# Attention weighting by seven half-wide products in place of eight, with x reread at the end of attention: one change to a fused attention and cluster-MLP kernel

## The chip, the cores and the metric

The kernel runs on one core of one Trainium2 chip. The metric is the device time of one execution in microseconds (us), as a median of several executions. The profile is that of one execution, taken by the hardware profiler. The engines are called by their short names: PE is TensorE's matmul (PEld is the load of its weights), DVE is VectorE, ACT is ScalarE, POOL is GpSimd, SP is SyncE, which here only issues DMAs. L513 is line 513 of the kernel before.

## The reference

Four images of 256 channels and 64 x 64 = 4096 positions go through two layers. The first is self-attention:

```python
q = jnp.einsum('oc,bcn->bno', wq, xf) + bq                  # 32 channels
k = jnp.einsum('oc,bcn->bon', wk, xf) + bk[None, :, None]   # 32 channels
attn = jax.nn.softmax(jnp.einsum('bnd,bdm->bnm', q, k), axis=-1)
v = jnp.einsum('oc,bcn->bon', wv, xf) + bv[None, :, None]   # 256 channels
out = jnp.einsum('bcn,bmn->bcm', v, attn).reshape(B, Cc, H, W)
return gamma[0] * out + x
```

The second layer normalises its input over the whole image (group norm with one group), adds a context-cluster block to it, normalises again, adds an MLP (256 to 1024, gelu, back to 256), and ends with two batch norms with relu and a 256 x 256 pointwise convolution between them. All is in float32.

The change is in the first layer: in the products of v with the softmax weights, in the addition of x, and in the statistics of the sum that the second layer needs.

## The kernel before, in words

**Stages.** Images are worked one after the other, each in three stages: attention (`weighting`, L619), the cluster block (`cluster`, L732) and the MLP (`mlp`, L1199). The order of instructions on every engine is the order in which the program writes them (`manual_schedule`); nothing reorders them. The projections of the next image (q, k and v from its x) are a list of small steps, which a "filler" hands out within the cluster block and the MLP of the image before. The next image's first eight units of scores are also made inside the MLP before it.

**Units.** Attention is divided into 8 blocks of 512 queries (`nb`) and 8 groups of 512 keys (`g`), so into 64 units `u = 8 nb + g`. A key group is four key tiles of 128. For each unit:

- `score` (L383): four matmuls, one for each key tile (L395), give scores of 128 keys x 512 queries. They lie in two PSUM buffers of two key tiles each (pool `ps_s`, L76). ACT copies both to an SBUF tile of the pool `spool` (L417, L422), and DVE takes a running maximum over the keys straight from PSUM (L421, L424; in group 0 one operation, L419).
- `exps` (L492): DVE subtracts the maximum (L500), ACT takes the exponential (L503), both in place, in two halves of two key tiles, and POOL adds the weights up in `acc` (L505, L508).
- `weigh` (L510): 16 recorded PE instructions of 512 columns (L513). A float32 matmul is recorded as two instructions; there are four key tiles and two halves of the channels (`KC`), so eight products. The sums stay in two PSUM banks `av` (pool `ps_a`, L77) over all eight groups of a block.

Scores are made ten units ahead (`LEAD`); ten slots of `spool` and one other tile hold them. What happens in which unit is written out by hand in `weighting`: each unit has four "quarters", one key tile each, and the table `at` (L606, L610) with `due` (L612) says in which unit and quarter the scores of a later unit are made. That is one unit's scores for one unit of weighting, except in an image's first six units, where the lead is caught up: there eight units' scores (seven in image 0) are due, one every 2.8 quarters (3 in image 0).

**Maximum and sum of a block.** The maximum of the next block is folded (`fold`, L429) and reduced across the partitions on DVE (`highest`, L473, called at the end of group 5), goes to DRAM and comes back as a row on all partitions (`everywhere`, L82), and is copied to a PSUM tile (`known`, L482, at the end of group 6), from which the subtractions read it. The sum of the weights of a finished block is taken in the same way in the next block (`gather`, L525; `total`, L532).

**Output of a block.** `clear` (L527) copies the two `av` banks to SBUF with the factor gamma. In the next block `add` (L541) multiplies by the reciprocal of the sum and adds x in place, both on POOL. x of the image lies in four tiles of `spool` throughout attention; ACT adds the bias gamma*bv to it once (`biased`, L622, L671). `seen` (L552) and `pooled` (L557) then take the statistics and the pooled cells that the cluster block needs, one block in each block of time. The tiles of the next image's x are loaded (`load_x`, L88) as slots come free, in the last units. For the last block the sum goes over PE (`den`, `inv`, from L686 on) with some filler steps between.

**PSUM.** There are eight banks: four in `ps_s` (two buffers of two banks), two in `ps_a`, two in `ps_m` (L78; maximum, projections and others).

Of the kernel before, what the change touches and what calls it, by code (L numbers as in the profile page):

```python
# [14 lines left out]
P = 128  # L15
B, C, H, W = 4, 256, 64, 64
N = H * W
# [13 lines left out]
LEAD, SLOTS = 10, 10  # L31

# [14 lines left out]
def attention_then_cluster_block(  # L47
# [23 lines left out]
    spool = ctx.enter_context(tc.tile_pool(name="spool", bufs=N // XT + SLOTS))  # L71
# [144 lines left out]
    def derived():  # L216
# [18 lines left out]
        tps = ps_m.tile([P, NB], F32, tag="m", name="wf_p")  # L235
# [50 lines left out]
    def attention(b, xs):  # L286
# [53 lines left out]
        def keys(i):  # L340

            ps = ps_m.tile([P, NB], F32, tag="m", name=f"kp_{b}_{i}")
            parts = [
                big.tile([P, NB], F32R, tag="k", bufs=2, name=f"hl{j}_{b}_{i}") for j in range(2)
            ]
            projected("k", i, ps)
            halves_of("k", i, *parts, ps)
# [35 lines left out]
        def score(u, hooks=None, later=None):  # L383

            nb, g = divmod(u, GRP)
            if u + 1 < units:
                k_unit(u + 1)
            q_s, k_s = qs[nb], ks.pop(u)
            pool, tag = (swap, "w1") if u % (SLOTS + 1) == SLOTS else (spool, "s")
            s = slots[u] = pool.tile([P, RG, NB], F32, tag=tag, name=f"s_{b}_{u}")  # L390
            halves = [
                ps_s.tile([P, 2, NB], F32, tag="s", name=f"sc_{b}_{u}_{h}") for h in range(2)
            ]
            for r in range(RG):
                nc.tensor.matmul(  # L395
                    halves[r // 2][:, r % 2, :],
                    k_s[:, r * P : (r + 1) * P],
                    q_s,
                    start=True,
                    stop=True,  # L400
                )
            if g == 0:
                tops[nb] = work.tile([P, 2, NB], F32, tag="top", bufs=1, name=f"top_{b}_{nb}")
            top = tops[nb]
            if hooks is not None:

                nc.scalar.copy(s[:, 0:2, :], halves[0])
                hooks.append(lambda: nc.scalar.copy(s[:, 2:4, :], halves[1]))
                for h in range(1 if g == 0 else 0, 2):
                    for i in range(2):  # L410
                        later.append(
                            lambda h=h, i=i: nc.vector.tensor_tensor(
                                top[:, i], s[:, i] if g == 0 else top[:, i], s[:, 2 * h + i], ALU.max
                            )
                        )
                return
            nc.scalar.copy(s[:, 0:2, :], halves[0])  # L417
            if g == 0:
                nc.vector.tensor_tensor(top, halves[1], s[:, 0:2, :], ALU.max)  # L419
            else:  # L420
                nc.vector.tensor_tensor(top, halves[1], top, ALU.max)  # L421
            nc.scalar.copy(s[:, 2:4, :], halves[1])  # L422
            if g:
                nc.vector.tensor_tensor(top, halves[0], top, ALU.max)  # L424
# [28 lines left out]
        def reduced(src, flipped, low, op):  # L453
# [4 lines left out]
            )  # L458
            four = low[:D, D : D + 64].rearrange("p (r c) -> p r c", r=4)
            for r in range(4):  # L460
                nc.vector.tensor_copy(four[:, r], low[r * D : (r + 1) * D, :16])
# [4 lines left out]
            return one  # L466
# [6 lines left out]
        def highest(nb):  # L473
# [3 lines left out]
            one = reduced(top[:, 0], top[:, 1], low, ALU.max)  # L477
# [4 lines left out]
        def known(nb, mb):  # L482
            mxs[nb] = ps_m.tile([P, NB], F32, tag="m", name=f"mb_{b}_{nb}")
            nc.scalar.copy(mxs[nb], mb)  # L484

        def spread(nb, dg):
            mxs[nb] = ps_m.tile([P, NB], F32, tag="m", name=f"mb_{b}_{nb}")
            nc.tensor.matmul(
                mxs[nb], ones, dg.rearrange("p j n -> p (j n)"), start=True, stop=True
            )  # L490

        def exps(u):  # L492
            nb, g = divmod(u, GRP)
            s = slots[u]
            if g == 0:
                accs[nb] = work.tile([P, 2, NB], F32, tag="acc", bufs=1, name=f"acc_{b}_{nb}")
            acc = accs[nb]
            for h in range(2):
                sh = s[:, 2 * h : 2 * h + 2, :]
                nc.vector.tensor_tensor(  # L500
                    sh, sh, mxs[nb].unsqueeze(1).to_broadcast([P, 2, NB]), ALU.subtract
                )
                nc.scalar.activation(sh, sh, AF.Exp)  # L503
            if g == 0:
                nc.gpsimd.tensor_tensor(acc, s[:, 0:2], s[:, 2:4], ALU.add)  # L505
            else:
                for h in range(2):
                    nc.gpsimd.tensor_tensor(acc, acc, s[:, 2 * h : 2 * h + 2], ALU.add)  # L508

        def weigh(u, av, quarter):  # L510
            g = u % GRP
            for c in range(KC):
                nc.tensor.matmul(  # L513
                    av[c],
                    own["v"][:, RG * g + quarter, c * P : (c + 1) * P],
                    slots[u][:, quarter, :],
                    start=(g == 0 and quarter == 0),
                    stop=(g == GRP - 1 and quarter == RG - 1),
                )
# [1183 lines left out]
```

## Time and profile before

| what | us |
|---|---|
| median of three runs | 3288.82 |
| lowest, highest of the three | 3286.51, 3291.25 |
| the profiled execution | 3289.97 |
| its span, from the first to the last instruction | 3287.9 |
| attention of image 0 (76.5 to 574) | 497.5 |
| cluster block of image 0 (574 to 655) | 81.0 |
| MLP of image 0 (655 to 890.5) | 235.5 |

Mean granted clock of PE: 0.994. Attention of images 1 to 3 takes 496.8, 493.5 and 523.0 (in the last a block of the image before is finished).

How to read the page: "busy" is time in which an engine executed; a share is of the span. A group line reads: line, engine, operation, output <- inputs, shape, count | busy us in all, mean ns of one | idle us of the engine just before them, and what ended most of it. The chain that ended last is followed back from the last instruction, at each step to what released it. In a timeline the columns are start, us from the first start to the last end of the instructions taken together, engine, line, and in brackets the idle time before and what ended it. PE's ends are modelled, since matmuls are pipelined: the distance between starts is the rate.

### The profile page before, as it was taken

To read this page: it belongs to the slowest core of one execution; us is meant where nothing else is said; L and a number is where in the kernel's file an instruction comes from. 1 tells how busy PE (TensorE), PEld (TensorE's weight loads), DVE (VectorE), ACT (ScalarE), POOL (GpSimd) and SP (SyncE) were. 2 spreads that over 40 slices of the span, in tenths; PEclk is the share of its full clock that TensorE was granted. 3 is DMA by queue.
4 is the path that set the end of the run, shared out by engine and by line. 5 is a ranking of instruction groups with operands and counts; after the bars stand their busy time and mean duration, and the time that the engine had idled before them with its cause. 6 is when DMAs were issued, how large, how long until landed. Compare 5 with 4: busy or idle time off the path is not lost.

```text
span 3287.9 us, 33084 instructions
## 1 busy us (share of the span) xinstructions
PE 3220.5 (98%) x11114; PEld 1933.6 (59%) x11114; DVE 2232.6 (68%) x3570; ACT 1680.7 (51%) x2254; POOL 1933.1 (59%) x1362
## 2 busy tenths in 40 slices
PE   7999999999999999999999999999999999999999
PEld 4444444788644444478864444457874444446786
DVE  3767774667677777467767776646776777765665
ACT  4655553445565555354556555434556555544444
POOL 0675676366456666636646567654654676673663
PEclk9999999999999999999999999999999999999999
DMA  4111113100111111310011111121011111110000
GB/s 159 52 42 49 49 39 114 36 20 30 42 52 40 47 55 33 114 36 20 30 52 45 48 52 42 45 98 36 30 37 51 51 42 48 45 44 1 14 20 26
DMA packets 87706, 154.78 MB, mean 47 GB/s; under 512 B 13200, under 2 KB 22000, under 8 KB 87536
## 3 DMA queue, kind: packets, MB, share of 16 engines
q1 hardware_dynamic: 86576, 151.55, 14.3%
q8 instruction: 88, 1.44, 0.2%
q10 hardware_dynamic: 832, 1.11, 0.1%
q14 instruction: 82, 0.67, 0.1%
q0 software_dynamic: 128, 0.00, 0.0%
HBM read 118.96 MB, written 33.67 MB: 46 GB/s over the span
## 4 chain that ended last, share of the span: by engine, by line
PE 93%; DVE 4%; ACT 1%; issue 1%; POOL 1%; DMA 0%; SPq 0%; ACTq 0%; DVEq 0%; POOLq 0%
PE av L513 52%; PE mo L1332 10%; PE sc L395 7%; PE hq L1415 5%; PE hp L1415 3%; PE hr L1415 3%; PE fv L911 3%; PE vp L358 3%; PE mo L1316 1%; PE hq_pw L1415 1%; PE pw L1271 1%; PE hr_pw L1415 1%; PE hp_pw L1415 1%; PE op L1023 1%; DVE hs L1406 0%
## 5 line engine op out<-in xcount | busy, mean ns | idle before, releaser
L513 PE MATMUL av<-s,v 128*128 128x512 f32 x4096 | 1796.3, 592 | 0.7 <-ACT s L503 0.7
L508 POOL TENSOR_TENSOR acc<-acc,s 128x1024 f32<-128x1024 f32 x448 | 1060.4, 2367 | 469.6 <-ACT s L503 449.0
L513 PEld LDWEIGHTS av<-s,v 128*128 128x128 f32 x4096 | 775.8, 190 | 896.4 <-issue 867.2
L503 ACT ACTIVATE s<-s 128x1024 f32<-128x1024 f32 x512 | 541.2, 1058 | 606.3 <-DVE s L500 586.0
L500 DVE TENSOR_TENSOR s<-s,mb 128x1024 f32<-128x1024 f32 x512 | 595.9, 1206 | 17.6 <-ACT mb L484 15.5
L421 DVE TENSOR_TENSOR top<-sc,top 128x1024 f32<-128x1024 f32 x196 | 239.2, 1221 | 290.8 <-PE sc L395 290.8
L1370 ACT ACTIVATE hs<-hs,pv_s 128x256 f32<-128x256 f32 x496 | 232.3, 502 | 344.5 <-DVE hs L1406 344.5
L395 PE MATMUL sc<-q,k 128*128 128x512 f32 x1024 | 373.1, 485 | 12.8 <-DMA k<-k 7.1
L1332 PE MATMUL mo<-hs,w 128*128 128x256 f32 x1512 | 385.4, 381 | 0.2 <-ACT hs L1370 0.2
L1332 PEld LDWEIGHTS mo<-hs,w 128*128 128x128 f32 x1512 | 283.9, 190 | 46.5 <-ACT hs L1370 7.0
L424 DVE TENSOR_TENSOR top<-sc,top 128x1024 f32<-128x1024 f32 x196 | 240.1, 1225 | 82.2 <-ACT s L417 69.1
L422 ACT COPY s<-sc 128x1024 f32<-128x1024 f32 x224 | 227.7, 1016 | 110.0 <-DVE top L421 73.8
L417 ACT COPY s<-sc 128x1024 f32<-128x1024 f32 x224 | 224.8, 1004 | 115.5 <-PE sc L395 87.4
L395 PEld LDWEIGHTS sc<-q,k 128*128 128x128 f32 x1024 | 191.9, 190 | 153.0 <-issue 113.6
L1406 DVE TENSOR_TENSOR hs<-hq,hs 128x256 f32<-128x256 f32 x496 | 198.8, 421 | 79.9 <-PE hq L1415 70.0
L505 POOL TENSOR_TENSOR acc<-s 128x1024 f32<-128x1024 f32 x32 | 76.0, 2374 | 243.6 <-ACT s L503 243.6
L1339 POOL TENSOR_TENSOR hs<-hs 128x256 f32<-128x256 f32 x108 | 82.3, 762 | 184.6 <-ACT hs L1423 95.2
L358 PE MATMUL vp<-wv_s,x 128*128 128x256 f32 x512 | 134.6, 411 | 10.8 <-DMA wv_s<-in_wv 8.8
L1406 DVE TENSOR_TENSOR hs<-hp,hs 128x256 f32<-128x256 f32 x124 | 52.2, 421 | 114.5 <-ACT hs L1423 114.5
L1415 PE MATMUL hr<-xn,w 128*128 128x256 f32 x496 | 128.4, 381 | 0.6 <-DVE hs L1406 0.6
L358 PEld LDWEIGHTS vp<-wv_s,x 128*128 128x128 f32 x512 | 100.8, 204 | 37.2 <-issue 14.7
L1415 PEld LDWEIGHTS hr<-xn,w 128*128 128x128 f32 x496 | 94.7, 191 | 18.2 <-issue 3.3
(271 smaller groups left out, 3503.1 us busy)
## 6 DMA issues: line engine op xcount, KB each, us to landing
k<-k SPq DMA_DIRECT2D x256, 256.0 KB, 2.8
out<-xn SPq DMA_DIRECT2D x62, 256.0 KB, 2.1
x<-in_x SPq DMA_DIRECT2D x30, 512.0 KB, 7.0
q<-q SPq DMA_DIRECT2D x32, 256.0 KB, 3.0
w<-in_w SPq DMA_DIRECT2D x8, 1024.0 KB, 10.6
mr<-row_mx SPq DMA_DIRECT2D x28, 256.0 KB, 3.7
rden<-row_rd SPq DMA_DIRECT2D x28, 256.0 KB, 3.7
q<-st_queries SPq DMA_DIRECT2D x24, 256.0 KB, 3.2
```

Source lines behind the costliest of these rows:

```text
L358: nc.tensor.matmul(vps[0][:, i % 2, :], xs[i * P // XT][:, k, o : o + P], wv_s[:, k, :], start=(k == 0), stop=(k == KC - 1),)
L395: nc.tensor.matmul(halves[r // 2][:, r % 2, :], k_s[:, r * P : (r + 1) * P], q_s, start=True, stop=True,)
L421: nc.vector.tensor_tensor(top, halves[1], top, ALU.max)
L424: nc.vector.tensor_tensor(top, halves[0], top, ALU.max)
L500: nc.vector.tensor_tensor(sh, sh, mxs[nb].unsqueeze(1).to_broadcast([P, 2, NB]), ALU.subtract)
L503: nc.scalar.activation(sh, sh, AF.Exp)
L508: nc.gpsimd.tensor_tensor(acc, acc, s[:, 2 * h : 2 * h + 2], ALU.add)
L513: nc.tensor.matmul(av[c], own["v"][:, RG * g + quarter, c * P : (c + 1) * P], slots[u][:, quarter, :], start=(g == 0 and quarter == 0), st ...
L1332: return nc.tensor.matmul(bank[:, half * HB : (half + 1) * HB], a[:, j], t, start=start, stop=stop)
L1370: nc.scalar.activation(src, src, AF.Gelu_apprx_tanh, bias=pvc("b1", P, j + 4 * (i > 1)))
L1406: nc.vector.tensor_tensor(dst, ps, term, ALU.add)
L1415: nc.tensor.matmul(out, w, x, start=True, stop=True)
```

## The change

**Seven products.** In the groups 0 to 6 the product of v and the weights is cut into 2 x 2 blocks: on the left v^T by channel halves and by pairs of key tiles (a11, a12, a21, a22), on the right the weights by the same pairs of key tiles and by halves of the 512 queries (B11, B12, B21, B22, of 2 key tiles x 256 queries). Seven products of such blocks take the place of eight, with sums of blocks as factors: three sums on the left (s2, s3, s4; a21 is replaced in place by a22 - a21), which are made once for an image on POOL and kept in three `spool` tiles ("sums"), and on the right three sums for each unit: `t31` on DVE (one operation of 128 x 1024), s12 and t4 on POOL (128 x 512 each). Each product has two key tiles of 256 columns in the middle dimension, so a unit has 28 recorded PE instructions of 256 columns. The products gather in four PSUM banks, the two of `ps_a` and both of `ps_m`. Group 7 is weighted plainly, 16 instructions of 512 columns, into two of the four banks, while ACT and POOL combine the other two (`clear`); after group 7 DVE adds the rest (`complete`).

**Sums of weights.** POOL no longer adds all four key tiles to `acc`; it builds two running sums (`one`, `both`) from `t31` and t4, two additions of 128 x 512 for a unit.

**PSUM for the maximum.** Since `ps_m` is taken, the maximum now lies in one of the two `ps_s` buffers (`hold`) through the whole attention, and the exponentials of B12 are written to the buffer's other bank. Scores are made in halves (`half`), half 0 before part 0 and half 1 before part 2 of a unit's products; ACT copies half by half, and DVE's running maximum comes for both halves from PSUM.

**Order.** `known` moves from the end of group 6 to the start of group 7, behind `clear` on ACT. `total` is cut into steps, in groups 1 to 3, its four small copies on ACT. In the first six units the halves have a table of their own.

**x and the residual.** x no longer stays in SBUF in attention. Finished blocks are multiplied by the reciprocal sum on POOL (`leave`) and written to DRAM (`att`). In the last ten units (`tail`) x and these blocks are read back, DVE adds both with the bias gamma*bv (`join`, one operation of 128 x 1024 or 128 x 512), and statistics and pooling of all blocks follow there. The next image's x is loaded in the same units.

**Moved besides.** The projection of q (`staged("queries")`, at the end of attention before) is now among the filler steps, cut in two; two weight preparations (`turn_mlp`, `turn_w2`) move from the end of attention into the cluster block. `load_mlp` comes two units before the end of attention (four for the last image). POOL's left-hand sums stand in the MLP of the image before (image 0: ahead of attention). `spool` has 13 buffers in place of 14.

The core of the diff:

```diff
+SEVEN = 7
+QW = NB // 2
+B21, B11, B12, B22 = range(4)
+PAIR = slice(B11, B12 + 1), slice(B21, B22 + 1, 3)
...
-    spool = ctx.enter_context(tc.tile_pool(name="spool", bufs=N // XT + SLOTS))
+    spool = ctx.enter_context(tc.tile_pool(name="spool", bufs=3 + SLOTS))
...
+        def products(u, h):
+
+            sc = ps_s.tile([P, 2, NB], F32, tag="s", name=f"sc_{b}_{u}_{h}")
+            k_s = ks[u]
+            for r in range(2):
+                nc.tensor.matmul(
+                    sc[:, r, :],
+                    k_s[:, (2 * h + r) * P : (2 * h + r + 1) * P],
+                    qs[u // GRP],
...
+        def kept(u, h, sc):
+            nc.scalar.copy(slots[u][:, PAIR[h]].rearrange("p h r n -> p r h n"), tiles(sc))
+
+        def half(u, h):
...
+            sc = products(u, h)
+            kept(u, h, sc)
             top = tops[nb]
...
+            if g:
+                return lambda: nc.vector.tensor_tensor(top, sc, top, ALU.max)
...
+        def known(mb):
+            nc.scalar.copy(own["hold"][:, 0], mb)
...
         def exps(u):
...
+            s = slots[u]
+            mb = own["hold"][:, 0].rearrange("p (h n) -> p h n", h=2).unsqueeze(2)
+            for j in range(2):
+                sh = s[:, PAIR[j]]
+                nc.vector.tensor_tensor(sh, sh, mb.to_broadcast([P, 2, 2, QW]), ALU.subtract)
+            if u % GRP < SEVEN:
+                b12 = own["hold"][:, 1].rearrange("p (r n) -> p r n", r=2)
+                nc.scalar.activation(b12, s[:, B12], AF.Exp)
+                nc.scalar.activation(s[:, B11], s[:, B11], AF.Exp)
+            else:
+                nc.scalar.activation(s[:, PAIR[0]], s[:, PAIR[0]], AF.Exp)
+            nc.scalar.activation(s[:, PAIR[1]], s[:, PAIR[1]], AF.Exp)
...
+        def factors(u):
...
+            nc.vector.tensor_tensor(
+                t31[u], s[:, B11 : B22 + 1 : 2], b12.to_broadcast([P, 2, 2, QW]), ALU.add
+            )
+            plus(s[:, B12], t31[u][:, 1], s[:, B11])
+            plus(t4s[u], s[:, B12], s[:, B21])
...
+                plus(one, t31[u - 1][:, 1] if g == 1 else one, t31[u][:, 1])
+                plus(both, both, t4s[u])
...
+            terms = {
+                1: (0, 0, a11, s[:, B11]),
+                5: (0, 1, a21, t31[u][:, 0]),
+                7: (1, 1, s3, t31[u][:, 1]),
+                2: (2, 0, a12, s[:, B21]),
+                6: (1, 0, s2, s[:, B12]),
+                4: (3, 0, a22, t4s[u]),
+                3: (2, 1, s4, s[:, B22]),
+            }
+            for i in ((1, 5), (7, 2), (6, 4), (3,))[part]:
+                bank, half_, a, t = terms[i]
+                for r in range(2):
+                    nc.tensor.matmul(
+                        av[bank][:, half_ * QW : (half_ + 1) * QW],
...
+            nc.scalar.activation(t[:, ::3], two(av[0]), AF.Identity, scale=pvc("gamma"))
+            nc.scalar.activation(t[:, 1:3], two(av[1]), AF.Identity, scale=pvc("gamma"))
+            plus(t[:, 1], t[:, 1], t[:, 0], ALU.subtract)
+            plus(t[:, 3], t[:, 1], t[:, 3], ALU.subtract)
+            plus(t[:, 1], t[:, 1], t[:, 2])
+            plus(t[:, 2], t[:, 2], t[:, 3])
...
+        def complete(nb, av):
...
+                nc.vector.scalar_tensor_tensor(dst, src, pvc("gamma"), dst, ALU.mult, op)
...
+        for u in range(6, units - LEAD):
+            due_at(u, 0, u + LEAD, 0)
+            due_at(u, 2, u + LEAD, 1)
+        for i in range(8 if b else 7):
+            q = (14 * i + 10) // 5, (14 * i + 17) // 5
+            if not b:
+                q = 3 * i + 2, (6 * i + 7) // 2
+            for h in range(2):
+                due_at(*divmod(q[h], RG), GRP + i + (b == 0), h)
...
+                for at_u, f in (
+                    (units - 10, lambda: (load(0), back(0))),
+                    (units - 9, lambda: load(1)),
+                    (units - 8, lambda: (add(0), back(1), load(2))),
+                    (units - 7, lambda: (seen(0), pooled(0), seen(1), load(3))),
+                    (units - 6, lambda: (pooled(1), add(1), back(2))),
+                    (units - 5, lambda: (seen(2), pooled(2), next_x(), next_x())),
+                    (units - 4, lambda: (seen(3), pooled(3), add(2), load_mix(b), next_x(), b == B - 1 and load_mlp(b))),
+                    (units - 3, lambda: (seen(4), pooled(4), seen(5), add_one(6), next_x(), begin())),
+                    (units - 2, lambda: (pooled(5), seen(6), pooled(6), b < B - 1 and load_mlp(b))),
...
+                maxima = due(u, 0)
+                if g == SEVEN:
+                    clear(nb, av)
+                if g == GRP - 1:
+                    gather(nb)
+                    if more:
+                        known(mb)
+                if g + 1 < GRP or more:
+                    exps(u + 1)
...
+                for f in maxima:
+                    f()
+                next(den, None)
                 weigh(u, av, 0)
-                due(u, 1)
+                for f in due(u, 1):
+                    f()
                 weigh(u, av, 1)
...
+                maxima = due(u, 2)
+                if g + 1 < GRP or more:
+                    factors(u + 1)
+                for f in maxima:
+                    f()
                 weigh(u, av, 2)
...
+                if nb and g == 1:
+                    den = total(nb - 1)
+                    next(den)
...
                 if g == GRP - 1 and more:
-                    clear(nb, av)
+                    complete(nb, av)
+                tail(u)
```

## The prediction

> **What bounds the kernel now.** I read the page's busy shares first, then the chain that ended last, then the costliest groups, then single stretches of the timeline.
>
> ```profile
> PE 3220.5 (98%) x11114; PEld 1933.6 (59%) x11114; DVE 2232.6 (68%) x3570; ACT 1680.7 (51%) x2254; POOL 1933.1 (59%) x1362
> ...
> PE 93%; DVE 4%; ACT 1%; issue 1%; POOL 1%; DMA 0%; SPq 0%; ACTq 0%; DVEq 0%; POOLq 0%
> ...
> L513 PE MATMUL av<-s,v 128*128 128x512 f32 x4096 | 1796.3, 592 | 0.7 <-ACT s L503 0.7
> ```
>
> TensorE is busy 98% of the span, carries 93% of the chain, and its largest group, the weighting, waited 0.7 us in all. So a TensorE instruction less is time less, as long as nothing else becomes late. Attention of image 0 lasts 497.5 us (76.5 to 574) with PE busy 495.6, DVE 341.4, ACT 264.9, POOL 329.9 (the windows view); the other images alike. The chain in order of time shows its beat, and PE's timeline inside the MLP shows what a 256-column product costs:
>
> ```profile
> 416.63 6.87 PE av L513 x16
> 423.50 0.93 PE sc L395 x4
> 424.43 6.87 PE av L513 x16
> ```
>
> ```profile
> 766.28 0.59 PE L1332 MATMUL mo<-hs,w 128*128 128x256 f32 x2
> 766.71 0.59 PE L1415 MATMUL hq<-xn,w 128*128 128x256 f32 x2
> 767.14 0.59 PE L1415 MATMUL hq<-xn,w_bac 128*128 128x256 f32 x2
> 767.58 0.59 PE L1415 MATMUL hq<-xn,w_bcd 128*128 128x256 f32 x2
> 768.01 1.03 PE L1332 MATMUL mo<-hs,w 128*128 128x256 f32 x4
> ```
>
> A unit (512 queries by 512 keys) is 7.79 us: 6.87 for 16 weighting instructions (0.429 each), 0.92 for four score instructions. Eight 256-column instructions take 768.01 − 766.28 = 1.73, so 0.216 each (the second column holds the last one's modelled end and is no beat). Now one unit's scores, in the timeline of all engines, lines of PE weights and POOL left out:
>
> ```profile
> 904.04 1.50 PE L395 MATMUL sc<-q,k 128*128 128x512 f32 x4
> ...
> 905.10 1.01 ACT L417 COPY s<-sc 128x1024 f32<-128x1024 f32 x1 [2.94 <-PE sc L395]
> ...
> 905.57 1.22 DVE L421 TENSOR_TENSOR top<-sc,top 128x1024 f32<-128x1024 f32 x1 [3.07 <-PE sc L395]
> ...
> 906.83 1.02 ACT L422 COPY s<-sc 128x1024 f32<-128x1024 f32 x1 [0.71 <-DVE top L421]
> 906.90 1.23 DVE L424 TENSOR_TENSOR top<-sc,top 128x1024 f32<-128x1024 f32 x1
> ...
> 908.04 2.34 DVE L500 TENSOR_TENSOR s<-s,mb 128x1024 f32<-128x1024 f32 x2
> ```
>
> Two things to see. ACT's copy of the second half starts when DVE's maximum of that same half ends: the two readers of a score buffer take turns (the waits list gives 73.8 us of it in 116 waits). And both buffers are free only at 908.1, four us after the scores; nobody minds, since the next scores come at 910.12.
>
> **The change, part by part.**
>
> *Seven products.* 56 of 64 units per image replace 16 × 0.429 = 6.87 by 28 × 0.216 = 6.05: 0.82 less, 46 per image, **−184**. The MLP rows already hold weight loads (190 ns) beside 0.216 instructions, so I take 0.216 for the new ones. New units: 6.05 + 0.92 = 6.97; group 7 stays 7.79.
>
> *One score buffer in place of two.* The maximum and the exponentials of B12 (`hold`) occupy one of the two score buffers through the whole attention, so halves are made one after the other: half 0 ahead of part 0, half 1 ahead of part 2, 3.45 us of products between. In the built program `half` is products → ACT copy → DVE maximum, the maximum waiting for the copy, and the next half's products for the maximum. By the rows: copy starts 0.66 after the products begin (904.04's four began at about 904.44, the copy at 905.10), copy 1.00, maximum 1.23, hand-overs 0.08: **2.97**. Half 1, at 3.91 in its unit, frees the buffer at 6.88; the next unit wants it at 6.97. Slack 0.09. The loop on DVE and ACT is as tight: maximum 1.15, two subtractions 2.27, exponentials of B12, B11 and pair 1 2.17 (they wait for both subtractions, since B12's go into `hold`), then `t31` 1.18: 6.77 of 6.97. PE is in order, so whatever DVE or ACT do beyond this stops it. Before, the same extras lay beside 7.79 us of weighting with two buffers ahead. I go through them by queue:
>
> - end of group 1 and group 2, `total`: transpose and reduce on DVE (0.70 + 0.69), then four small copies on ACT ahead of half 1's copy (0.84): 1.75 late.
> - end of group 5, `fold` and `highest` (0.69 + 0.70 + 0.69 + 0.84 + 0.45 = 3.4 on DVE), less what lies beside part 3 and the slack: 1.8.
> - group 7: ACT does half 0's copy, two `clear` copies of PSUM (0.6 each) and `known` (0.5) ahead of the subtractions, which need `known`; half 0's maximum is behind both subtractions: 7.0 where 3.9 is wanted, 3.1.
> - `complete`, three DVE operations from PSUM (0.475 to 0.75) behind group 7's last product; next unit's half 0 maximum is behind them: 1.6.
>
> 8.3 per block, for the six blocks in which scores are still being made: 6 × 4 × 8.3 = **+199**. The 16 halves due in the first six units come closer together, and at odd parts ACT's exponentials (two of 1.06) stand ahead of the copy: two stalls of 4.4, the others 1 to 1.7: 17.7 per image, 14 in image 0: **+67**.
>
> *x reread, residual at the end.* Before, POOL adds, statistics and pooling (`seen`, `pooled`) were spread over seven blocks. Now all of them come in units 54 to 63, where no scores are made. DVE's loop without maxima is about 5.5 a unit; units 56 to 62 make 38.5, plus 25.1 of extras: adds 6 × 1.23 and 2 × 0.75, `total` 2.05, statistics 12 × 0.68, pooling 5 × 1.21. 63.6 on DVE against 42.3 on PE: 21.3 per image, **+85**. The traffic (10 MB per image more: x again, and 3 MB of attention out and back) runs at 7.0 us per 512 KB on queues that are 0.19 busy; SP issues it behind nothing urgent (keys and queries landed 2.8 to 3.2 us after issue, the rows of the maximum 3.7, and are asked for a unit or more ahead): 0, and if a 1 MB piece came late, its 7 to 10.6 us would show once per image in DVE's adds, not on PE.
>
> *Sums of values and weights.* POOL's per-unit accumulations (2 × 2.37) become four additions of 1.27: no longer. The 28 left-hand sums per image (0.75 to 0.8) stand in the preceding MLP, where POOL is busy 131 of 235.5 us: I take 1 us, but 0 to 21 is possible, since `hs` L1339 on POOL feeds TensorE there.
>
> *Ends.* The last block's denominators wait for POOL's group 7 sums (+2.7). The next image's `t31` stands on DVE ahead of `last`'s subtraction (+2.4). The queries' projection (3.64 us of PE at 563.42) moves into the fillers of cluster and saves about its waits (−1). With the MLP's 1: **+20** over four.
>
> *PE's clock.* Sum above: nothing. The row: four score instructions behind an idle 3.73 took 2.05, without it 1.27.
>
> ```profile
> 42.32 2.05 PE L395 MATMUL sc<-q,k 128*128 128x512 f32 x4 [3.73 <-DMA k<-k]
> ...
> 48.85 1.27 PE L395 MATMUL sc<-q,k 128*128 128x512 f32 x4
> ```
>
> Also behind a 2.36 gap at 625 the granted clock fell to 0.50 for some 3 us, but not behind two gaps of 2.35 (1438, 2247). With 24 stalls of 3.1, 0 to 40 us: into the range.
>
> [...]
>
> **Sum.** −184 + 199 + 67 + 85 + 20 = +187, on the profiled execution's 3289.97 (span 3287.9 and 2.07 around it; 0.03% above the median 3288.82): **3477 us**. The terms' own ends: block stalls 5 to 10 each (120 to 240), first units 40 to 90, end 60 to 100, MLP to +20 × 3: **3380 to 3540** for this case.
>
> **Rivals.**
>
> *A: the buffer comes back in time.* If maximum and copy of a half overlap in fact, or start sooner, and a half is free after about 2 us in place of 2.97, slack is over 1 us in every unit and swallows all lumps but group 7's. Left are 18 + 2 + 10 + 5 per image: −184 + 140 = −44: **3246**. For it: ACT and DVE are only 51 and 68% busy. Against: 906.83 starts on DVE's end, and one buffer has nothing to alternate with. It decides from a chain under 2 us. Chance 0.20.
>
> *B: only the taking of turns is milder.* Then DVE's lumps stay: 4.4 per block, 2 in the first units, 15.5 at the end, 5 around: −184 + 106 + 8 + 62 + 20 = +12, **3302**. Chance 0.14.
>
> *C: the steady unit doesn't fit.* The slack of 0.09 is worked out from rows with simpler layouts. 0.3 us more, in strided copies or a weight load that shows between 256-column products, stops PE in each of about 200 steady units: +60, **3534**. For it: PEld's 190 ns beside 216. Against: the MLP keeps 0.216. The change not doing what it says (256-column products that are no cheaper per column) lies here too. Chance 0.18.
>
> The forecast has 0.48.
>
> **How the numbers follow.** Faster by over 0.2% (6.6 us, about what measuring this kernel can tell): A and a fifth of B, 0.24. Within: 0.05 of B. Slower: the rest, 0.71. For 8 in 10 the range runs from A's time, leaving half of A below, to 3550, leaving half of C above.
>
> **What would show it.** Right: in steady units `av` plus score 6.97 to 7.0, PE's attention idle 60 to 100 us per image, released by DVE's maximum (`top`) and ACT's copies; stalls near 3 in group 7, near 1.8 at the end of groups 1 and 5; the last ten units some 20 us longer than their products. Seven products show as 0.216 a piece. A: PE idle under 35 us per attention. C: every unit above 7.2. Wrong altogether: if PE waits for the DMA of x or k, or if the loss lies in the MLP.

## The result, and the profile after

The changed kernel takes 3638.85 us as a median of four runs (3628.91 to 3663.36), against 3289.3 before: the ratio is 1.107 (95% interval 1.102 to 1.113). The forecast was 3477 and the range ended at 3550, so the direction was right and the size, +187 against +350, was not. The four times go with the granted clock: 0.961 in the shortest, 0.952 in the longest. The profiled execution is the longest of the four (3663.36, span 3661.5); what follows is about it.

The page after, in the lines that answer to those of before (busy shares, chain by engine), and the group of the score products from the list by line (instructions | busy, mean ns of one | idle time ahead of them, and what ended it):

```profile
PE 3238.7 (88%) x13866; PEld 2514.7 (69%) x13866; DVE 2622.9 (72%) x3778; ACT 1690.8 (46%) x2594; POOL 2233.5 (61%) x2150
...
PE 40%; DVE 24%; POOL 13%; ACT 11%; issue 8%; DMA 4%; SPq 0%; ACTq 0%; DVEq 0%; POOLq 0%
```

```profile
L406 PE MATMUL sc<-q,k 128*128 128x512 f32 x1024 | 406.1, 484 | 278.4 <-DVE top L431 153.9 <-DMA k<-k 89.8 <-DVE few L494 15.6
```

TensorE has lost the chain: 40% of it in place of 93%. Most of its idle time stands ahead of the score products, and the list names three things that end it: DVE's maximum (154 us), loads of keys (90 us), DVE's reduction (16 us). The 16 us are five waits in group 5, where the other blocks wait for keys; they go with the keys' waits in the first experiment. One block of image 0 on PE's timeline, some of the score products of its second half and group 7's products:

```profile
285.46 0.81 PE L406 MATMUL sc<-q,k 128*128 128x512 f32 x2
...
292.47 0.81 PE L406 MATMUL sc<-q,k 128*128 128x512 f32 x2
...
299.18 0.70 PE L406 MATMUL sc<-q,k 128*128 128x512 f32 x2 [3.31 <-DMA k<-k]
...
308.01 0.70 PE L406 MATMUL sc<-q,k 128*128 128x512 f32 x2 [1.63 <-DMA k<-k]
...
315.13 1.19 PE L406 MATMUL sc<-q,k 128*128 128x512 f32 x2 [2.99 <-DVE top L431]
316.12 4.66 PE L610 MATMUL av<-s,v 128*128 128x256 f32 x10
```

A unit without extras lasts 292.47 − 285.46 = 7.01. Then come a wait of 3.31 and one of 1.63 for keys, and 2.99 in group 7 for the maximum. (Group 7 is recorded as 14 instructions of 512 columns and 4 of 256, not as the 16 of 512 in the account of the change; the last line merges both widths.)

From the starts of each unit's first `av` product I take the length of every unit. Means of blocks 1 to 5 over the four images, beside what the prediction's lumps make of them (6.97 or 7.79 and the lump):

| group | 0 | 1 | 2 | 3 | 4 | 5 | 6 | 7 | block |
|---|---|---|---|---|---|---|---|---|---|
| before | 7.79 | 7.79 | 7.79 | 7.79 | 7.79 | 7.79 | 7.79 | 7.79 | 62.3 |
| forecast | 8.57 | 6.97 | 8.72 | 6.97 | 6.97 | 6.97 | 8.77 | 10.9 | 64.8 |
| after | 8.08 | 7.00 | 8.70 | 7.02 | 7.00 | 10.44 | 9.24 | 12.55 | 70.0 |

First block 66.2 before, 90.6 after; last block 58.0 and 74.5. In sum attention goes from 495.6 to 576.5 per image (+324 in all), and the stretches between from 1305.7 to 1355.7 (+50). Groups 0 to 4 are within 0.5 of the forecast. The surplus is in groups 5 to 7.

### The profile page after: what moved, and what is told of

Its sections match the earlier page's. It is cut to its first block, busy times and chain, and to the rows that moved or that the text cites. A ratio compares the mean times of both kernels' runs of the same rounds, so it can differ in the third digit from the quotient of the medians.

```text
span 3661.5 us, 40440 instructions
## 1 busy us (share of the span) xinstructions
PE 3238.7 (88%) x13866; PEld 2514.7 (69%) x13866; DVE 2622.9 (72%) x3778; ACT 1690.8 (46%) x2594; POOL 2233.5 (61%) x2150
## 4 chain that ended last, share of the span: by engine, by line
PE 40%; DVE 24%; POOL 13%; ACT 11%; issue 8%; DMA 4%; SPq 0%; ACTq 0%; DVEq 0%; POOLq 0%
PE mo L1535 9%; DVE s L539 7%; POOL acc L549 6%; PE hq L1618 4%; PE av L632 4%; DVE t L569 4%; PE sc L406 3%; POOL t L549 3%; PE av L610 3%; DVE top L431 3%; PE hp L1618 3%; ACT s L546 3%; POOL s L549 3%; PE hr L1618 3%; PE fv L1113 2%
## 5 line engine op out<-in xcount | busy, mean ns | idle before, releaser
L549 POOL TENSOR_TENSOR s<-t,s 128x512 f32<-128x512 f32 x224 | 289.6, 1293 | 714.9 <-DVE t L569 649.2
L539 DVE TENSOR_TENSOR s<-s,hold 128x1024 f32<-128x1024 f32 x512 | 598.6, 1210 | 116.2 <-ACT hold L523 114.1
L431 DVE TENSOR_TENSOR top<-sc,top 128x1024 f32<-128x1024 f32 x392 | 478.7, 1221 | 95.5 <-ACT s L419 93.2
L632 PE MATMUL av<-s,v 128*128 128x256 f32 x1792 | 482.2, 393 | 33.7 <-ACT s L543 33.7
L632 PE MATMUL av<-t,v 128*128 128x256 f32 x1792 | 492.2, 399 | 21.5 <-DVE t L569 17.6
L632 PE MATMUL av<-s,sum 128*128 128x256 f32 x1792 | 468.9, 385 | 0.0
L549 POOL TENSOR_TENSOR acc<-acc,t 128x512 f32<-128x512 f32 x352 | 457.0, 1318 | 0.0
L632 PEld LDWEIGHTS av<-s,v 128*128 128x128 f32 x1792 | 351.4, 197 | 101.2 <-ACT s L543 41.7
L632 PEld LDWEIGHTS av<-t,v 128*128 128x128 f32 x1792 | 356.3, 200 | 88.7 <-DVE t L569 31.7
L632 PEld LDWEIGHTS av<-s,sum 128*128 128x128 f32 x1792 | 346.6, 193 | 56.8
L549 POOL TENSOR_TENSOR t<-s 128x512 f32<-128x512 f32 x224 | 300.9, 1343 | 35.0 <-PE av L632 17.9
```

The lines of the kernel that those rows point to most:

```text
L431: return lambda: nc.vector.tensor_tensor(top, sc, top, ALU.max)
L539: nc.vector.tensor_tensor(sh, sh, mb.to_broadcast([P, 2, 2, QW]), ALU.subtract)
L549: nc.gpsimd.tensor_tensor(out, x, y, op)
L632: nc.tensor.matmul(av[bank][:, half_ * QW : (half_ + 1) * QW], a[:, r], t[:, r], start=(g == 0 and r == 0 and i in (1, 7, 2, 4)), stop=(g ...
```

## Experiments

All kernels start from the changed one unless said otherwise. Times are medians; the kernel before ran beside each at 3288.7 to 3290.1.

### Keys' load ahead of SP's waits

```diff
-            if u + 1 < units:
+            if u + 1 < units and u + 1 not in ks:
                 k_unit(u + 1)
...
+                if (nb and g == 4 or g == 5) and u + 12 < units:
+                    k_unit(u + 12)
                 if nb and g == 4:
                     leave(nb - 1)
```

SP's timeline of the changed kernel, in the block shown above, is the reason for the edit:

```profile
280.90 0.39 SPq L389 DMA_DIRECT2D k<-k  x1
294.89 0.88 SPq L700 DMA_DIRECT2D att<-t  x2
295.87 0.40 SPq L389 DMA_DIRECT2D k<-k  x1
```

The write of the finished block waits for POOL's multiplication (292.48 to 294.86), and the next keys, 15 us behind the keys before them, are issued behind it.

> Edit: the load of the next keys is issued on SP just ahead of the two things in a block on which SP waits (the write of a finished block at the end of group 4, the rows of the maximum at the end of group 5); nothing else moves. Theory S (SP's queue, the step that the prediction put at nothing): PE's 83 us of waits for k in the four attentions go, units of group 5 fall from 10.4 to about 7.0, and with them some of the half-clock periods: 3639 becomes 3530 to 3560. Rival D: the loads are late by chance of the same moment, and DVE's fold and highest at the end of group 5 hold PE there anyway: group 5 stays above 9, time above 3610.

Measured (run e1_k_first): 3619.9, 19 less. No wait for k is left in attention and group 5 is 7.01, but group 6 grows from 9.24 to 12.47: both theories were half right. Under the wait for keys lay a second one nearly as long. DVE's and PE's timelines of this kernel show it:

```profile
1180.81 1.02 DVE L467 TENSOR_TENSOR top<-top 128x512 f32<-128x512 f32 x1
1181.86 0.71 DVE L493 STREAM_TRANSPOSE top<-top 128x512 f32<-128x512 f32 x1
1182.60 0.69 DVE L494 TENSOR_REDUCE few<-top 128x16 f32<-128x512 f32 x1
1183.33 3.46 DVE L500 COPY few<-few 32x16 f32<-32x16 f32 x4
...
1187.24 2.30 DVE L539 TENSOR_TENSOR s<-s,hold 128x1024 f32<-128x1024 f32 x2
```

```profile
1184.65 0.80 PE L406 MATMUL sc<-q,k 128*128 128x512 f32 x2
1192.84 1.22 PE L406 MATMUL sc<-q,k 128*128 128x512 f32 x2 [4.80 <-DVE top L434]
```

The prediction had 3.4 for `fold` and `highest` with 0.84 for the four copies. They take 3.46, the whole 6.4, and the subtractions stand behind it. In group 7 the wait is only 0.5 to 1.1 here in most units, since the products ahead of it run at half clock (eight of 512 columns in 6.11, where the changed kernel at full clock took 3.60), and the unit lasts 11.07.

### The copies of the maximum's reduction on ACT

```diff
-            *_, one = reduced(top[:, 0], top[:, 1], low, ALU.max)
+            *_, one = reduced(top[:, 0], top[:, 1], low, ALU.max, nc.scalar.copy)
```

The same copies in the lists by line, of the kernel before and after (mean ns of one behind the comma; the 224 of before serve both reductions, the 112 of after the maximum alone):

```profile
L461 DVE COPY few<-few 32x16 f32<-32x16 f32 x224 | 52.7, 235 | 4.2
```

```profile
L500 DVE COPY few<-few 32x16 f32<-32x16 f32 x112 | 85.8, 766 | 2.1
```

The traces settle what makes them long. In the changed kernel 76 of the 112 copies began while an instruction of POOL ran; they took 1.05 in the mean, and every one ended 0.02 to 0.03 us behind the end of a POOL instruction. The other 36, with POOL idle at their start, took 0.16. In the kernel before the same two kinds are 33 (0.65) and 191 (0.16).

> Edit: e1_k_first, and the four copies of 32x16 in the reduction of a block's maximum on ACT in place of DVE. In the profile of after these copies take 0.77 each on DVE (0.235 before), and a long one ends 0.14 plus its own 0.16 behind the end of an instruction of POOL. Theory P (a DVE copy waits for POOL's running instruction, and this made the lump at the end of group 5 6.4 long where the prediction had 3.4): the stall of 4.8 in group 6 falls to 2 to 2.5, against e1_k_first's 3620 the time falls by 50 to 70, to 3550 to 3570. Rival A: ACT's copies come as late as DVE's or delay ACT's own chain: within 15 of 3620.

Measured (e7_highest_act): 3598.8, 21 less than with the keys alone. (The expectation misreads the trace in one number: a long copy ends 0.03 behind POOL's instruction.) The wait of 4.80 falls to 1.77 and group 6 to 9.40, 0.6 above the 8.77 of the forecast, so theory P is right on the place. But group 7 rises from 11.09 to 12.91: behind the shorter wait in group 6 the wait of 2.99 in group 7 is back, with a half-clock period behind 19 of the 24. So the total was less than half of the least I expected.

### PE kept busy in its waits

```diff
+        def kept_warm(u, part, av):
+            for _ in range(warm.get((u, part), 0) // 2):
+                nc.tensor.matmul(av[3][:, :QW], zeros, own["v"][:, 0], start=False, stop=False)
...
+                kept_warm(u, 2, av)
                 maxima = due(u, 2)
```

Two group 7 units of the changed kernel with the same wait, on PE's timeline, the first pair at half clock (a unit of 13.94), the second at full clock (11.03):

```profile
244.03 1.19 PE L406 MATMUL sc<-q,k 128*128 128x512 f32 x2 [2.99 <-DVE top L431]
245.02 6.07 PE L610 MATMUL av<-s,v 128*128 128x256 f32 x10
...
384.61 0.70 PE L406 MATMUL sc<-q,k 128*128 128x512 f32 x2 [2.99 <-DVE top L431]
385.14 3.60 PE L610 MATMUL av<-s,v 128*128 128x256 f32 x10
```

> Edit: ahead of the score products that wait longest (groups 6 and 7 of six blocks, two places in the first block) PE does 6 to 20 extra instructions of 256 columns with a zero left factor into an open bank, as long as the wait lasts; they add nothing to the result, and the waits themselves stay. Theory C (clock): the half-clock periods behind these stalls go, from 70 in the profile to about 30; group 7 units become 11.0 everywhere in place of 11.0 to 14.1, and the time falls by 60 to 100, to 3540 to 3580. Rival I: the low periods lie mostly in idle time and cost little: less than 20 us of change, or slower by the added work.

Measured (e2_warm): 3611.6, 27 less. The half-clock periods in the clock's records fall from 70 to 29 and every group 7 unit is 11.03, as theory C has it; the time falls by less than half of the least it had. One reason is in the units of e1_k_first above: where PE waits again some microseconds later, slower products only shorten that wait (a unit of 11.07 at half clock, 11.03 at full clock).

### All three together

The three edits above, the extra products only where waits are left.

> Edit: e7_highest_act (keys' load ahead of SP's waits, copies of the maximum's reduction on ACT), and PE kept busy with products of a zero left factor in the waits that are left: 8 instructions in group 6 and 14 in group 7 of six blocks, 18 each in units 2 and 3 of images 1 to 3. So the three terms that the prediction put at nothing or too small (SP's queue, DVE's copies behind POOL, the clock) are out, all others in. Theory: what is left is near the forecast's own sum of 3477, and group 7 units are 11.0 everywhere: 3500 to 3540. Rival: something else of 100 us is still in it, the clock is worth no more than in e2_warm (27): 3565 or more.

Measured (e12_three_terms): 3537.6, 101 less. Blocks 1 to 5 are now 8.08, 7.00, 8.69, 7.00, 7.00, 7.00, 9.41, 11.03: 65.2, where the forecast had 64.8. In these blocks the three terms are all but 0.4 of the error of 5.2. What is left to 3477 is mostly elsewhere: the first block 87.0, the last 74.8, the stretches between 1352.3. In image 0 the first block is 95.5, in the others 84: there small preparations run on DVE, and one of their tiles (`wf_p`) takes the score buffer too, so the next scores wait 3.4 us (4.35 in the changed kernel) for it.

### Exponentials in place

```diff
-            if u % GRP < SEVEN:
-                b12 = own["hold"][:, 1].rearrange("p (r n) -> p r n", r=2)
-                nc.scalar.activation(b12, s[:, B12], AF.Exp)
-                nc.scalar.activation(s[:, B11], s[:, B11], AF.Exp)
-            else:
-                nc.scalar.activation(s[:, PAIR[0]], s[:, PAIR[0]], AF.Exp)
+            nc.scalar.activation(s[:, PAIR[0]], s[:, PAIR[0]], AF.Exp)
...
-            b12 = own["hold"][:, 1].rearrange("p (r n) -> p r n", r=2).unsqueeze(1)
+            b12 = s[:, B12].unsqueeze(1)
```

> Edit: the exponentials of B12 stay in the unit's own SBUF tile, one ACT operation of 128x1024 with B11 in place of two, and t31 reads them from there; the buffer hold is only read for the maximum. Theory L (the closed loop on DVE and ACT: maximum, both subtractions, exponentials, t31, 6.8 of 7.0 us): the first exponential no longer waits for the second subtraction, the loop falls to about 5.7 and swallows lumps of up to 1 us: group 2 from 8.7 to about 7.2, group 0 from 8.07 to 7.3, the last ten units 7 us per image shorter: 3639 becomes 3520 to 3570. Rival H: the half chain of one score buffer (2.97, slack 0.09) is what stalls PE, or t31 from SBUF is slower: groups 0 and 2 stay within 0.3 of what they are, time above 3610.

Measured (e4_in_place): 3586.8, 52 less. Group 0 falls to 7.71, group 2 to 7.83, the last block to 66.6: the loop of DVE and ACT was tight, and ends sooner now. `t31` takes 1.44 from SBUF in place of 1.22 from PSUM, which gives part of it back; theory L had the direction and three quarters of the least it expected.

### The three cures, and the order in group 7

> Edit: e1_k_first, e4_in_place and the copies on ACT together. If SP's order, the closed loop and the DVE lump are separate causes in one row: groups 5 and 6 together 16 to 17 in place of 19.7, group 7 about 10.5 to 11, block 1 to 5 some 64; 3639 becomes 3460 to 3510. If they hide one another: not below 3530.

Measured (e9_three): 3502.5, 136 less, at the upper end of the times expected if the causes add, and more than the 19 + 21 + 52 = 92 of the single steps. Groups 5 and 6 sum to 17.0; group 7 is 12.03, above the 10.5 to 11 that was expected.

```diff
+                late = g == SEVEN and more and len(maxima) > 0
+                if late:
+                    known(mb)
                 if g == SEVEN:
                     clear(nb, av)
...
+                if late:
+                    exps(u + 1)
+                    for f in maxima:
+                        f()
+                    maxima = []
```

> Edit: e9_three, and in group 7 of a block in which scores are made: the row of the maximum is copied ahead of the two copies of clear, DVE's maximum of half 0 stands ahead of the subtractions, and ACT's copy of half 1 ahead of the exponentials. Theory Q (order of ACT's and DVE's queues makes the 3 us of group 7, as the prediction worked out): group 7 falls from about 11.0 to 8 to 8.5, some of it given back in group 0; 3 us or more per block, with a half-clock period behind each: 70 to 100 us less than e9_three. Rival L2: the lump is a sum of DVE and ACT work that only moves on to group 0: less than 30.

Measured (e10_g7_order): 3463.3, 39 less. Group 7 is 7.80 in every block, as theory Q says, and group 0 rises from 7.71 to 10.28: rival L2 names what became of the rest. Group 0 now has one wait of 1.98 and two lengths. PE's timeline in two such units:

```profile
1026.40 0.73 PE L406 MATMUL sc<-q,k 128*128 128x512 f32 x2 [1.98 <-DVE top L431]
...
1027.84 1.03 PE L627 MATMUL av<-t,v 128*128 128x256 f32 x4
...
1089.45 0.76 PE L406 MATMUL sc<-q,k 128*128 128x512 f32 x2 [1.98 <-DVE top L431]
...
1090.93 1.91 PE L627 MATMUL av<-t,v 128*128 128x256 f32 x4
```

> Edit: e10_g7_order with such products in the waits of units 2 and 3 (14 each, images 1 to 3), group 0 and group 6 (8 each). In e10_g7_order a group 0 unit with the same wait of 1.98 lasts either 9.4 or 11.05. Theory C: the 1.7 are the clock, all group 0 units become 9.4 and the first block 3 to 5 us shorter: 3463 becomes 3425 to 3445. Rival: the two lengths come from something else (DVE or ACT): both lengths stay, less than 10 us of change.

Measured (e13_g7_warm): 3442.2, 21 less, and group 0 is 9.40 in the mean (9.0 to 9.7, 10.28 before): the 1.7 us were the clock. The clock's records say the same: in e10_g7_order each of the long units holds a half-clock period of 3.41, here none does. This is the fastest version of the changed kernel found, and 4.7% slower than the kernel before (4.5 to 4.8).

```diff
+                after = u < 6 and (u, 1) in at
...
+                if after:
+                    exps(u + 1)
```

> Edit: e10_g7_order, and in the first six units, where a half of scores is due at part 1, subtractions and exponentials stand behind that half's copy and maximum. Theory Q: the two stalls of 4 per image in units 2 and 3 fall under 2, with them a half-clock period each: 15 to 35 us less than e10_g7_order over four images. Rival: the sixteen halves are too much for DVE and ACT in six units, whatever the order: less than 8, or slower.

Measured (e11_six_order): 3498.5, 35 more than without. The first block goes from 82.0 to 88.5. In e10_g7_order the waits of units 2 and 3 were already down to 3.05 (4.15 and 3.9 in the changed kernel); here they are 3.3 and 2.5, and new ones of 2.5 and 3.5 come in units 4 and 5. So this order is no cure; whether another is stays open.

### The last ten units

> Edit: in the last ten units the six additions of the reread x and attention tiles move from DVE (scalar_tensor_tensor, 1.23 each) to POOL (two key halves of 128x1024), the bias to ACT. Theory E (DVE sets the last ten units): 7.4 us per image less, 3639 becomes 3605 to 3615. Rival P: POOL, with four additions per unit, becomes late in its place: no change, or slower.

Measured (e6_joins_pool): 3630.5, 8 less, which is within the spread of the changed kernel's runs; the last block stays 73.7. POOL became late in DVE's place: the statistics on DVE now wait 7.6 us per image for it.

> Edit: the changed kernel without the six additions of the attention output to the reread x in units 56 to 60 of each image (the output lacks these parts); all loads stay. They took 1.84 each on DVE in the profile of after, where the prediction had 1.23. Theory E (DVE sets the last units): 11 us per image less, 3639 becomes 3585 to 3605. Rival X: ACT and POOL, whose exponentials and sums wait there too, hold the same time: less than 15.

Measured (e14_no_joins): 3586.4, 52 less, the last block 65.3 in place of 74.5: 37 us over four images; the rest of the 52 lies outside these units. DVE's additions stand in the way here, as the prediction had it, and cost more than its 1.23 each. But DVE is not full: it is busy 80% of the last block's first seven units and waits there 15 us per image for ACT's exponentials. It is the closed loop of DVE and ACT that sets these units, and e4_in_place, which takes no work from DVE, shortens the block nearly as much (to 66.6). The additions in the list by line:

```profile
L714 DVE SCALAR_TENSOR_TENSOR x<-x,gbv,tb 128x1024 f32<-128x1024 f32 x24 | 43.3, 1844 | 0.0
```

### One score buffer in the kernel before

```diff
+            sc = ps_s.tile([P, 2, NB], F32, tag="s", name=f"sc_{b}_{u}_{h}")
...
+            own["hold"] = ps_s.tile([P, 2, NB], F32, tag="s", name=f"hold_{b}")
...
+        for u in range(6, units - LEAD):
+            due_at(u, 0, u + LEAD, 0)
+            due_at(u, 2, u + LEAD, 1)
```

> Edit to the kernel before: the maximum lies in one of the two score buffers through attention, scores are made in halves in the other at the changed kernel's places, and nothing else (eight products, x in SBUF, all other work in its place). Theory B1 (one buffer alone is harmless at a beat of 7.79, for its loop has about 1 us to spare; the loss comes with the shorter beat): steady units stay 7.79, only DVE's larger lumps show, 10 to 70 us in all: 3300 to 3360. Rival B2: the single buffer costs as much as in the changed kernel, 24 blocks of 8 us and the first units: 3450 or more.

Measured (e15_one_buffer): 3473.2, 184 more than the kernel before. My theory B1 fell: units without extras are 7.78, but groups 0, 1, 6 and 7 are 10.14, 8.68, 9.10 and 8.65, and the first block 80.6. Group 0 on DVE's and PE's timelines:

```profile
1021.98 0.70 DVE L474 STREAM_TRANSPOSE few<-rden 128x512 f32<-128x512 f32 x1
1022.71 0.69 DVE L475 TENSOR_REDUCE few<-few 128x16 f32<-128x512 f32 x1
1023.43 2.78 DVE L480 COPY few<-few 32x16 f32<-32x16 f32 x4
...
1026.93 1.17 DVE L440 TENSOR_TENSOR top<-sc,top 128x1024 f32<-128x1024 f32 x1
```

```profile
1028.16 0.73 PE L430 MATMUL sc<-q,k 128*128 128x512 f32 x2 [1.88 <-DVE top L440]
```

Here too the copies are long, and the maximum stands behind them. The next pair of runs has them on ACT, with one buffer and with two:

> Edit: e15_one_buffer (the kernel before with one score buffer) with the small copies of both reductions on ACT. In e15_one_buffer the four copies took 2.8 on DVE behind POOL's additions in group 0. Theory P (much of what one buffer costs are these copies, which nothing hides any more): groups 0 and 1 fall from 18.8 to 16.5 or less, 3473 becomes 3390 to 3430. Rival B2 (the buffer itself): less than 25.

> Edit: the kernel before, two score buffers, with the same copies on ACT and nothing else. By every theory the second buffer hides DVE's copies there: within 0.2% of 3289.

Measured: 3412.3 (e17_one_buffer_act) and 3287.9 (e18_before_act, ratio 0.9994, 0.9985 to 1.0003). Groups 0 and 1 sum to 16.2, as theory P has it. With two buffers the copies cost nothing, with one 61 us. With the copies out of the way the buffer costs 3412.3 − 3289.4 = 123, of which some 58 lie in the four first blocks (80.6 in place of 66.2).

### The second buffer given back

```diff
-            nc.scalar.copy(own["hold"][:, 0], mb)
+            own["mb"] = mb
...
-            mb = own["hold"][:, 0].rearrange("p (h n) -> p h n", h=2).unsqueeze(2)
+            mb = own["mb"].rearrange("p (h n) -> p h n", h=2).unsqueeze(2)
```

> Edit: e9_three (keys' load ahead, exponentials of B12 in place, copies on ACT), and the maximum is subtracted from its SBUF row, so that hold and the copy to it go and both score buffers serve the scores; still halves, seven products. Theory O (giving up the second score buffer is what costs, as e15_one_buffer's 180 us say; clock and queues are its consequences): waits of PE for DVE's maximum nearly vanish, blocks 1 to 5 fall from 65 to 58 to 60, the first block to 70 to 74: 3502 becomes 3340 to 3390. Rival T (the lumps are DVE's throughput; with two SBUF inputs the subtractions slow down from 1.21 to 1.45 and DVE is full): 3430 to 3500.

Measured (e16_two_buffers): 3702.0, 199 more than the three cures with one buffer: rival T, and worse than it said. The subtractions in the lists by line, changed kernel and this one:

```profile
L539 DVE TENSOR_TENSOR s<-s,hold 128x1024 f32<-128x1024 f32 x512 | 598.6, 1210 | 116.2 <-ACT hold L523 114.1 <-PE hold L529 2.1
```

```profile
L541 DVE TENSOR_TENSOR s<-s,mr 128x1024 f32<-128x1024 f32 x512 | 988.6, 1969 | 24.9 <-DMA mr<-row_mx 19.6 <-ACT mr L533 4.4
```

With both inputs in SBUF a subtraction takes 1.97 in place of 1.21, and POOL's additions beside it 1.90 in place of 1.32. DVE is busy 93% of blocks 1 to 5 (80% with one buffer), so the run can't say what a second buffer would bring where nothing else changes; in the changed kernel that stays open. One sign that it would bring something: the first block, where scores come closest together, falls from 86.8 to 76.4 in spite of the slower subtractions. What the run does say is what it costs to take the maximum out of PSUM.

## Why the prediction was right in direction and wrong in size

- **Seven products, −184: right.** Units without extras are 7.00 (6.97 forecast). Rival C, a steady unit that doesn't fit, did not happen.
- **One buffer's chain and loop: right.** The wait in group 7 is 2.99 (3.1), group 2 gains 1.70 (1.75), group 0 only 1.08 (1.6), the two long waits of the first units 4.15 and 3.9 (4.4). Rivals A and B, a buffer that comes back sooner, did not happen.
- **`fold` and `highest` "3.4 on DVE": mis-sized.** They took 6.4, for 76 of the 112 copies began while POOL was at work and ended only 0.02 to 0.03 behind the end of one of its instructions. I took the row of before, 0.84 for four, made where POOL mostly left gaps (191 of the 224 copies). The subtraction behind it was off as well: 3.4 less what lies beside part 3 (4 × 0.216 = 0.86) and the slack of 0.09 is 2.4, not 1.8, and 2.4 is what group 6 keeps with the copies on ACT (9.40 − 7.00).
- **"SP issues it behind nothing urgent": wrong.** The keys' loads are issued behind the write of a finished block, which waits for POOL. That made 83 us of waits in the four attentions; alone they were worth only 19, for DVE's lump stood behind.
- **"PE's clock. Sum above: nothing": wrong.** There were 70 half-clock periods in place of 10. The nothing was my estimate, and no run shows it: in the changed kernel a half-clock period followed 23 of 31 waits of 2.5 to 3.0, and in e10_g7_order 13 of 26 waits of 1.95 to 2.01. The prediction's own row, the clock at 0.50 behind a gap of 2.36, had pointed this way. The bound of 40 was an estimate too, put into the range for group 7 alone (24 stalls, each behind it some 3 us at 0.50 as in that row, would lose 36). Keeping PE busy was worth 27 in the changed kernel, and 61 (3598.8 − 3537.6) where the other two terms were gone.
- **The three together:** 101 of the 162 us between forecast and measurement.
- **The end, +85: right in kind, a little small.** The last block is 74.5 where the sum has some 70; the additions took 1.84 in place of 1.23.
- **Ends, +20: too small.** The stretches outside attention grew by 50, of which 11 are the moved projection (3 × 3.64).

The direction was no luck: the stalls behind the single buffer came where the prediction put them, and nearly in its sizes. The range failed since each of the three terms was costed at its cheap end. It was also narrower than its own parts: the terms' upper ends, added up, make −184 + 240 + 90 + 100 + 20 + 60 = +326, which is 3616, or 3656 with the 40 for the clock, while the range ended at 3550.

Behind it all: seven products save 184, and what they need, four PSUM banks for the sums, takes the second score buffer, which is worth 123 to 184 us to the kernel before. That is shown for the kernel before; that the buffer is worth as much in the changed kernel is not shown. The rest, sums on DVE and POOL and x's return at the end, comes on top. No version of the changed kernel beats the kernel before.

## What to carry to other kernels

Where a scheme with fewer products needs PSUM that double-buffered another stage, price the lost buffer first: list everything on the engines that read it, for here the work beyond the slack stopped TensorE (154 us of waits for DVE's maximum in the changed kernel). In queues that are worked in order, look for every instruction that waits, a DMA issue that waits for a slow engine among them, and ask what stands behind it. Where several waits end within a few microseconds of one another, the removal of one shows its own worth only after the others are gone; test them together as well as alone.

## What the runs showed of the hardware

- DVE's small SBUF copies were longer beside POOL. In the changed kernel copies of 32x16 took 0.16 where POOL was idle at their start (36) and 1.05 where it was at work (76), and each of the 76 ended 0.02 to 0.03 us behind the end of one of POOL's instructions. Subtractions with the maximum in SBUF (e16_two_buffers) took 1.97 against 1.21 with it in PSUM (the changed kernel), and `t31` with both inputs in SBUF (e4_in_place) 1.44 against 1.22.
- Of the changed kernel's 70 half-clock periods of PE 36 lasted 3.41 us and 33 lasted 6.83; of the 10 of the kernel before six and three. They came behind waits under 3 us too. In the changed kernel a period began during or within 3.4 us after 23 of the 31 waits of 2.5 to 3.0 us, 14 of the 22 of 3.0 to 3.5, and all 15 of 4 to 7. In e10_g7_order it did so for 13 of the 26 waits of 1.95 to 2.01 us, and for none of the 29 of 1.7 to 1.9.
